# Causal attention in a transformer block: the 256-column parts of two neighbouring groups of heads share a unit

## The chip, the cores and the metric

The kernel runs on one core of a Trainium2 chip. The metric is the device time of one execution in microseconds (us); several executions give a median. A profile is one further execution in which every instruction of each engine was recorded. The engines are TensorE (PE; its weight loads are shown as PEld), VectorE (DVE), ScalarE (ACT), GpSimd (POOL) and SyncE (SP), which issues the transfers. "L1372" is line 1372 of the kernel.

## The reference

Eight sequences of 1024 tokens with 512 features go through one transformer block whose normalizations are modulated by a condition. Cut to what matters:

```python
mod = silu(condition) @ Wada + bada
sh_a, sc_a, gt_a, sh_m, sc_m, gt_m = split(mod, 6, axis=1)
xm = layernorm(x, g1, be1) * (1 + sc_a) + sh_a
q, k, v = split_heads(xm @ Wqkv)                    # 16 heads of 32
scores = einsum('bhqd,bhkd->bhqk', q, k) * 32 ** -0.5
scores = where(causal, scores, -inf)
x = x + gt_a * (softmax(scores) @ v @ Wproj + bproj)
xm = layernorm(x, g2, be2) * (1 + sc_m) + sh_m
x = x + gt_m * (gelu(xm @ W1 + b1) @ W2 + b2)
```

All inputs and the output are float32. The causal mask lets a token see itself and what is before it.

## The kernel before

**Tiling.** The 8 sequences are cut in two halves of 512 tokens, which gives 16 blocks n = (b, h). A block with h = 0 attends to its own keys, one with h = 1 also to those of the half before it. The 16 heads of 32 features are four groups g of four heads. A group's queries and keys lie with features on the partitions, 32 for each head, so its four heads are multiplied at once on four row tiles of TensorE (32 rows, 128 columns: the forms "32*128"). The linear layers, the values and the sums use four column tiles instead ("128*32"), and the transposes the whole array ("128*128"). float32 matmuls show as two instructions each in the trace.

**Units of attention.** The scores are made twice. A *score unit* (scores, here mostly scores_at_once, L1372) has queries on the partitions. It fills the PSUM tile "st" of four heads by 512 columns; VectorE adds the mask on the diagonal squares (L1384) and takes the maximum of each row (L1392). When a group's last score unit is done, split_maxima splits its maxima into three bf16 numbers (four small operations, L1411 to L1414, on VectorE or GpSimd, as the planner decides), and maxima_rows lays them out as a row (TensorE L1430, ScalarE copy L1436). A *weight unit* (weights_T) has keys on the partitions: the products again (L1456), then the maxima are subtracted by bf16 matmuls with a row of minus ones (L1467), ScalarE takes the exponential (L1479) into one of three SBUF buffers pT, and GpSimd zeroes what lies above the diagonal (affine_select, L1484). weigh multiplies by the values into the PSUM tile "po" (L1507), and additions (L1611, some on VectorE in the last group, L1608) gather the weights into the group's first pT, from which finish makes the sums (L1525), their reciprocals and the quotient. Scores and weights share the one PSUM tile "st", so each unit waits until the engine that reads the one before it is done.

**The triangle.** On the diagonal block of 512 by 512 only the lower triangle of 128-wide strips is computed. Its four strips have 512, 384, 256 and 128 columns and are packed in three units: [0], [1, 3] and [2], that is 512, 384 + 128, and 256 alone (TRIANGLE). A group has three units of each kind in a block with h = 0, and seven (four full ones first) with h = 1.

**Order.** Nothing is scheduled by the compiler: the program is written out in order by a planner at build time. It keeps an estimated clock per engine (now), and for each buffer when it is written and left (note, note_pe, note_act). Linear work (projections q, k, v, output projection, the two MLP layers, all Strassen products) runs as threads of small steps; before an attention unit, step_aside lets such steps go first while the unit would wait, and pace sets how far the linear work should be. attend walks through slots: slot k of group g makes weight unit k, closes the unit before it (values and, at the end, the sums), adds weights, and then makes as many score units of the next group as `upto` says. The buffers' queue free_p hands out three pT; a group's first one is kept until its sums are made. SyncE issues weight pieces in the order in which the linear steps will need them, as buffers of a ring of nine come free, with the loads of x, of the gate rows (row_ga and others, L493) and the stores between them. The output projection (project_out) of block n takes its first gate product on VectorE from row_ga.

Of the kernel before, what the change touches and what calls it, by code (L numbers as in the profile page):

```python
# [22 lines left out]
def kernel(  # L23
# [33 lines left out]
    nc = tc.nc  # L57
# [829 lines left out]
    def project_out(n):  # L887
# [8 lines left out]
        if last:  # L896
            for t in range(NTT):
                written["att", n, t] = NEVER
# [379 lines left out]
    def score_units(n, g):  # L1278

        h = blocks[n][1]  # L1280
        whole = [[(qt, kh, 0, TB)] for kh in range(h) for qt in range(NTT)]
        for tri in TRIANGLE:
            parts, at = [], 0
            for i in tri:
                w = TB - i * P
                parts.append((NTT - 1 - i, h, at, w))
                at += w
            whole.append(parts)
        return [(n, g, parts) for parts in whole]

    def weight_units(n):

        h = blocks[n][1]
        whole = [[(k, 0, TB)] for k in range(h * NTT)]
        for tri in TRIANGLE:
            parts, at = [], 0
            for i in tri:
                parts.append((h * NTT + i, at, TB - i * P))
                at += TB - i * P
            whole.append(parts)  # L1300
        return whole
# [13 lines left out]

    def scores(n, g, parts):

        h = blocks[n][1]
        if (n, g) not in maxima:
            maxima[n, g] = small.tile([P, 2, NTT, HPG], F32, tag="mx", name=f"mx_{n}_{g}")  # L1320
        mx = maxima[n, g]
        reads = [("qT", n), ("kT", n - h + parts[0][1])]
        if (
            linear_wait() > 3000
            and not any(live)
            and wait_of((reads, ["st"])) > wait_of((reads, [BANK])) + 1000
        ):
            scores_by_heads(n, g, parts, mx, reads)
        else:
            scores_at_once(n, g, parts, mx, reads)  # L1330
        if units[unit_at[0] + 1 :] == [] or units[unit_at[0] + 1][:2] != (n, g):
            split_maxima(n, g, h)

    def scores_by_heads(n, g, parts, mx, reads):

        h = blocks[n][1]
        for some in (range(HPG - 1), range(HPG - 1, HPG)):
            step_aside(reads, [BANK])
            of = {j: lin_bank() for j in some}
            for qt, kh, c0, w in parts:  # L1340
                for j, bank in of.items():
                    r = slice(j * hd, (j + 1) * hd)
                    nc.tensor.matmul(
                        banks[bank][:, c0 : c0 + w],
                        qTs[n][r, g, ts(qt, P)],
                        keys_of(n, kh)[r, g, :w],
                        start=True,
                        stop=True,
                        skip_group_check=True,
                    )  # L1350
                note_pe(2 * COLUMN * w, "rows", reads, [("l", bank) for bank in of.values()])
            for j, bank in of.items():
                if parts[0][1] == h:
                    first, span = parts[0][3] - P, len(parts) * P
                    diagonal = banks[bank][:, first : first + span]
                    nc.vector.tensor_tensor(diagonal, diagonal, mask[:, :span], ALU.add)
                    note("DVE", 120 + 1.04 * span, [("l", bank)])
                for qt, kh, c0, w in parts:
                    nc.vector.tensor_reduce(
                        mx[:, kh, qt, j : j + 1], banks[bank][:, c0 : c0 + w], axis=AX.X, op=ALU.max  # L1360
                    )
                    note("DVE", 170 + w, [("l", bank)], [("mx", n, g)])
                live[bank] = False

    def scores_at_once(n, g, parts, mx, reads):
# [3 lines left out]
        for qt, kh, c0, w in parts:  # L1369
            for j in range(HPG):  # L1370
# [3 lines left out]
                    qTs[n][r, g, ts(qt, P)],  # L1374
                    keys_of(n, kh)[r, g, :w],
# [5 lines left out]
        if parts[0][1] == h:  # L1381
            first, span = parts[0][3] - P, len(parts) * P
            diagonal = sc[:, :, first : first + span]
            nc.vector.tensor_tensor(  # L1384
                diagonal,
                diagonal,
                mask[:, :span].unsqueeze(1).to_broadcast([P, HPG, span]),
                ALU.add,
            )
            note("DVE", 165 + 4.16 * span, ["st"])  # L1390
        for qt, kh, c0, w in parts:
            nc.vector.tensor_reduce(  # L1392
                mx[:, kh, qt, :], sc[:, :, c0 : c0 + w], axis=AX.X, op=ALU.max
            )
            note("DVE", 170 + 4.14 * w, ["st"], [("mx", n, g)])
# [48 lines left out]
    def weights_T(n, g, parts):  # L1444
# [3 lines left out]
        row = m_rows[n, g]  # L1448
        reads = [("qT", n), ("kT", n), ("mrow", n, g)]
        step_aside(reads, ["st"])  # L1450
        st = ps_st.tile([P, HPG, TB], F32, tag="st", name=f"st_{n}_{g}_{parts[0][0]}")
        for k, c0, w in parts:
            kT = keys_of(n, k // NTT)
            for j in range(HPG):
# [3 lines left out]
                    kT[r, g, ts(k % NTT, P)],  # L1458
                    qT[r, g, TB - w :],
# [4 lines left out]
        for k, c0, w in parts:  # L1464
# [16 lines left out]
        if parts[0][0] >= h * NTT:  # L1481
            for _, c0, _ in parts:
# [13 lines left out]
    def weigh(n, g, parts, pT, slot, last):  # L1496
# [6 lines left out]
        for k, c0, w in parts:  # L1503
# [61 lines left out]

    def attend():
        previous = None
        for n in range(NB):
            h = blocks[n][1]
            t_units = weight_units(n)  # L1570
            n_slots = len(t_units)
            slots = []
            mine = sum(exp_need(parts) for parts in t_units) * NC
            for g in range(NC):
                nxt = groups.index((n, g)) + 1
                for k in range(n_slots):
                    upto = len(units)
                    if nxt < len(groups):
                        lo, m = first_unit[groups[nxt]], len(score_units(*groups[nxt]))
                        upto = lo + min(m, -(-(k + 2) * m // n_slots))  # L1580
# [4 lines left out]
                    slots.append((g, k, upto))  # L1585
            mine += sum(score_need(*unit) for unit in units[unit_at[0] : slots[-1][2]])
# [3 lines left out]
            for g, k, upto in slots:  # L1590
                parts = t_units[k]
# [8 lines left out]
                if k > 0:  # L1600
                    acc, first = totals[n, g]
                    for _, c0, w in parts:
                        for j in range(HPG):
                            into = acc[:, j, TB - w :]
                            keys = [("p", slot)], [("acc", n, g), ("p", first)]
                            if j % 2 and (n, g) == groups[-1]:

                                nc.vector.tensor_tensor(into, into, pT[:, j, c0 : c0 + w], ALU.add)  # L1608
                                note("DVE", 150 + 2 * w, *keys, port=True)
                            else:  # L1610
                                nc.gpsimd.tensor_tensor(into, into, pT[:, j, c0 : c0 + w], ALU.add)  # L1611
                                note("POOL", 230 + 2.07 * w, *keys)
# [16 lines left out]
    def close(n, g, parts, pT, slot, last):  # L1629

        until(lambda: n - blocks[n][1] + parts[-1][0] // NTT in valued)
        weigh(n, g, parts, pT, slot, last)
        if parts[0][0] == 0:
            totals[n, g] = (pT, slot)
        else:
            free_p.append(slot)
# [15 lines left out]
    def score_need(n, g, parts):  # L1652
        ns = 300 + sum(100 + 2100 * w / TB for _, _, _, w in parts)
# [3 lines left out]
    needs = sum(exp_need(parts) for n in range(NB) for parts in weight_units(n)) * NC  # L1657
    needs += sum(score_need(*unit) for unit in units)
    for n in range(NB):
# [5 lines left out]
        if n > 2:  # L1665
            written["free for k", n] = NEVER
    normalize(x_pre.pop(0), "a0", [("x", "a0")] * NTT)
# [67 lines left out]
```

## Time and profile before

| | |
|---|---|
| median of three runs | 3648.94 us (3645.09 to 3651.8) |
| the profiled execution | 3647.89 us |
| its span, first to last instruction | 3646.2 us |
| mean granted TensorE clock | 0.995 |
| exponentials of 2048 and of 1024 elements | 256 and 64, mean 1.879 and 1.025 us |
| reductions of 2048, 1536, 1024 and 512 elements | 191, 63, 64 and 63, mean 2.291, 1.758, 1.225 and 0.681 us |
| additions of weights, 512, 384, 256 and 128 columns (GpSimd) | 504, 254, 254 and 254, mean 1.308, 1.045, 0.750 and 0.459 us |

The span is what the trace covers; the time of an execution lies a little above it. In the profile a group of instructions is one line, engine, operation and set of tiles, with the count, the busy time, the mean of one in ns, and the idle time of its engine just before it. A wait belongs to the instruction that came last to release it. Matmuls overlap in the pipeline, so the time that one takes is read from start to start, not from its length.

### The profile page before, as it was taken

Reading aid. Unit: us, or ns where it says so; the run is one execution under the profiler, and the core shown is the slowest. Engines: PE = TensorE matmul, PEld = TensorE weight load, DVE = VectorE, ACT = ScalarE, POOL = GpSimd, SP = SyncE. Lnnn points to the kernel's source line nnn. Section 1 sums busy time; section 2 is a strip of 40 time slices with the busy share of each in tenths; the row PEclk is TensorE's granted clock in tenths of the full one; section 3 lists DMA queues with packets and bytes.
Section 4 is the critical chain, followed back from the end, with each engine's and each line's share of the span. In section 5 each row is a group of like instructions: output and inputs, shape, how many; then the busy total and the mean of one; then the engine's idle time right before and its main releaser. Section 6 shows DMA issues by size and latency. Waiting matters only on the chain. (4 is left out here: it accounts for less than half of the span.)

```text
span 3646.2 us, 121167 instructions
## 1 busy us (share of the span) xinstructions
PE 3571.6 (98%) x54821; PEld 1770.1 (49%) x54821; DVE 2179.1 (60%) x2501; ACT 1329.2 (36%) x1413; POOL 2014.6 (55%) x2039
## 2 busy tenths in 40 slices
PE   8999999999999999999999999999999999999999
PEld 4434445445554455544545444454544545445445
DVE  6766675564746557465564656746667465664663
ACT  2335234252333523335242352424524244241431
POOL 3656645656455664566636665456654566544560
PEclk9999999999999999999999999999999999999999
DMA  6623333333333343433434334343333433334334
GB/s 220 225 92 104 104 103 109 123 106 119 114 115 112 106 126 111 134 94 104 126 106 143 91 100 123 106 137 103 97 122 110 140 100 103 117 97 143 92 107 138
DMA packets 307894, 430.35 MB, mean 118 GB/s; under 512 B 25900, under 2 KB 176236, under 8 KB 307380
## 3 DMA queue, kind: packets, MB, share of 16 engines
q1 hardware_dynamic: 307264, 422.56, 37.9%
q8 instruction: 432, 7.08, 0.8%
q14 instruction: 82, 0.67, 0.1%
q10 hardware_dynamic: 116, 0.03, 0.0%
HBM read 394.12 MB, written 28.38 MB: 116 GB/s over the span
## 5 line engine op out<-in xcount | busy, mean ns | idle before, releaser
L1611 POOL TENSOR_TENSOR pT<-pT,pT 128x512 f32<-128x512 f32 (+3 forms) x1266 | 1189.2, 973 | 524.9 <-ACT pT L1479 377.1
L1479 ACT ACTIVATE pT<-st 128x2048 f32<-128x2048 f32 (+1 forms) x320 | 546.5, 1708 | 951.3 <-PE st L1467 909.0
L201 PE MATMUL bank<-w,hT 128*32 128x256 f32 x14336 | 808.6, 380 | 2.8 <-DVE hT L1006 2.1
L1392 DVE TENSOR_REDUCE mx<-sc 128x4 f32<-128x1024 f32 (+3 forms) x381 | 664.4, 1757 | 192.4 <-PE sc L1372 185.8
L201 PEld LDWEIGHTS bank<-w,hT 128*32 128x32 f32 x14336 | 452.1, 110 | 354.0 <-issue 58.0
L201 PE MATMUL bank<-xm_m,w 128*32 128x256 f32 x8192 | 506.6, 380 | 0.6 <-ACT rec L1531 0.5
L1484 POOL TENSOR_SCALAR_AFFINE_SELECT pT<-pT 128x512 f32<-128x512 f32 x256 | 175.3, 696 | 576.9 <-ACT pT L1479 576.9
L201 PE MATMUL bank<-t_m,w 128*32 128x256 f32 x6144 | 383.2, 380 | 0.9 <-ACT hT L188 0.9
L201 PEld LDWEIGHTS bank<-xm_m,w 128*32 128x32 f32 x8192 | 253.3, 110 | 252.0 <-issue 98.0
L1456 PE MATMUL st<-qT,kT 32*128 32x512 f32 (+3 forms) x3072 | 339.6, 526 | 21.0 <-DVE mx L1392 20.0
L1372 PE MATMUL sc<-kT,qT 32*128 32x256 f32 (+3 forms) x3048 | 340.6, 527 | 2.9 <-DVE mx L1392 1.9
L1384 DVE TENSOR_TENSOR sc<-sc,mask 128x1024 f32<-128x1024 f32 (+1 forms) x191 | 166.7, 873 | 248.5 <-PE sc L1372 225.5
L1507 PE MATMUL po<-pT,v 128*32 128x512 f32 (+3 forms) x3072 | 312.7, 493 | 2.2 <-POOL pT L1484 1.2
L201 PEld LDWEIGHTS bank<-t_m,w 128*32 128x32 f32 x6144 | 191.9, 110 | 175.7 <-issue 54.2
L201 PE MATMUL bank<-xm_a,w 128*32 128x256 f32 x3968 | 243.5, 381 | 0.0
L201 PE MATMUL bank<-w,qT 128*32 128x512 f32 x2048 | 241.1, 597 | 0.4 <-DVE qT L1547 0.2
L1540 DVE RECIPROCAL rec<-rec 128x128 f32<-128x128 f32 x256 | 224.6, 919 | 8.5 <-ACT rec L1531 8.5
L1456 PEld LDWEIGHTS st<-qT,kT 32*128 32x128 f32 x3072 | 128.9, 184 | 182.7 <-issue 57.5
L1372 PEld LDWEIGHTS sc<-kT,qT 32*128 32x128 f32 x3048 | 126.8, 184 | 161.0 <-ACT pT L1479 77.4
L193 DVE TENSOR_TENSOR hT<-bank,u_u 128x512 f32<-128x512 f32 x192 | 130.2, 686 | 120.9 <-PE bank L201 116.7
L201 PE MATMUL bank<-t_a,w 128*32 128x256 f32 x2944 | 187.2, 382 | 0.0
L1479 ACT ACT_TABLE_LOAD x89 | 114.2, 1283 | 189.3 <-PE st L1467 188.6
(205 smaller groups left out, 3589.5 us busy)
## 6 DMA issues: line engine op xcount, KB each, us to landing
w<-in_L_cond_W_dram SPq DMA_DIRECT2D x384, 256.0 KB, 2.9
w<-kept_up_S SPq DMA_DIRECT2D x256, 256.0 KB, 2.6
w<-kept_down_S SPq DMA_DIRECT2D x256, 256.0 KB, 2.7
w<-kept_qkv_S SPq DMA_DIRECT2D x180, 256.0 KB, 3.0
w<-in_L_cond_Wqkv_dram SPq DMA_DIRECT2D x147, 256.0 KB, 3.3
hat<-in_x_dram SPq DMA_DIRECT2D x64, 256.0 KB, 3.2
w<-in_L_cond_Wproj_dram SPq DMA_DIRECT2D x64, 256.0 KB, 3.8
xr<-in_x_dram SPq DMA_DIRECT2D x64, 256.0 KB, 4.2
```

What stands on the lines that cost most here:

```text
L193: nc.vector.tensor_tensor(out, src, other, op)
L201: nc.tensor.matmul(ps[r, :], lhsT[:, r], rhs, start=start, stop=stop, skip_group_check=True)
L1372: nc.tensor.matmul(sc[:, j, c0 : c0 + w], qTs[n][r, g, ts(qt, P)], keys_of(n, kh)[r, g, :w], start=True, stop=True, skip_group_check=True,)
L1384: nc.vector.tensor_tensor(diagonal, diagonal, mask[:, :span].unsqueeze(1).to_broadcast([P, HPG, span]), ALU.add,)
L1392: nc.vector.tensor_reduce(mx[:, kh, qt, :], sc[:, :, c0 : c0 + w], axis=AX.X, op=ALU.max)
L1456: nc.tensor.matmul(st[:, j, c0 : c0 + w], kT[r, g, ts(k % NTT, P)], qT[r, g, TB - w :], start=(c0 == 0), stop=False, skip_group_check=True,)
L1479: nc.scalar.activation(pT[:, :, :used], st[:, :, :used], AF.Exp, scale=scale)
L1484: nc.gpsimd.affine_select(diagonal, diagonal, pattern=[[0, HPG], [1, P]], compare_op=ALU.is_ge, fill=0.0, base=0, channel_multiplier=-1,)
L1507: nc.tensor.matmul(po[r, TB - w :], v[:, k % NTT, g * P + j * hd : g * P + (j + 1) * hd], pT[:, j, c0 : c0 + w], start=(k == 0), stop=last ...
L1540: nc.vector.reciprocal(some, some)
L1611: nc.gpsimd.tensor_tensor(into, into, pT[:, j, c0 : c0 + w], ALU.add)
```

## The change

The third unit of the triangle, 256 columns, is no longer a unit of its own in each group. Groups with even g make one unit of 512 columns out of their own 256 and those of group g + 1, for the scores and for the weights; groups with odd g have one unit fewer of each kind. A part carries its group as a last entry. In the shared score unit the mask reaches the diagonal squares of both parts in one operation (diagonals), and each part has its own reduction. In the shared weight unit each part subtracts the maxima of its own group, so the row of group g + 1 must be there by then; attend makes its score units one slot earlier in even groups (`over`), and calls for the row if it isn't made. One exponential takes both parts. The values and the additions of the second part are kept in `shared` and done when the first unit of group g + 1 is closed, and the pT buffer is freed only then. The mark that the last block's quotients aren't written yet is set at the start. Row counts of the planner (mine, needs) follow. The diff without the changes that only carry the new entry along:

```diff
@@ score_units
-        whole = [[(qt, kh, 0, TB)] for kh in range(h) for qt in range(NTT)]
+        whole = [[(qt, kh, 0, TB, g)] for kh in range(h) for qt in range(NTT)]
...
+            if tri == [2]:
+                if g % 2:
+                    continue
+                parts.append((*parts[0][:2], at, w, g + 1))
             whole.append(parts)
@@ weight_units(n, g)
+            if tri == [2]:
+                if g % 2:
+                    continue
+                parts.append((parts[0][0], at, TB - 2 * P, g + 1))
             whole.append(parts)
@@
+    def diagonals(parts, sc):
+        if parts[-1][4] == parts[0][4]:
+            first, span = parts[0][3] - P, len(parts) * P
+            return span, sc[:, :, first : first + span]
+        return 2 * P, sc.rearrange("p j (a c) -> p j a c", c=2 * P)[:, :, :, P:]
@@ scores_at_once
+            span, place = diagonals(parts, sc)
+            shape_of = mask[:, :span].unsqueeze(1)
+            if len(place.shape) == 4:
+                shape_of = shape_of.rearrange("p o (a c) -> p o a c", c=P)
+            nc.vector.tensor_tensor(place, place, shape_of.to_broadcast(place.shape), ALU.add)
...
+        for qt, kh, c0, w, gg in parts:
+            nc.vector.tensor_reduce(
+                maxima[n, gg][:, kh, qt, :], sc[:, :, c0 : c0 + w], axis=AX.X, op=ALU.max
+            )
@@ weights_T
-        reads = [("qT", n), ("kT", n), ("mrow", n, g)]
+        reads = [("qT", n), ("kT", n)] + [("mrow", n, gg) for gg in {part[3] for part in parts}]
@@ attend
+                n_slots = len(weight_units(n, g))
+                over = n_slots - 1 if g % 2 == 0 else n_slots
...
-                        upto = lo + min(m, -(-(k + 2) * m // n_slots))
+                        upto = lo + min(m, -(-(k + 2) * m // over))
...
+                parts = weight_units(n, g)[k]
+                while rows_due and any((n, part[3]) not in m_rows for part in parts):
+                    maxima_rows()
                 pT, slot = weights_T(n, g, parts)
...
+                    add_weights(n, g, [part for part in parts if part[3] == g], pT, slot)
@@ close
-        weigh(n, g, parts, pT, slot, last)
+        own, other = [[part for part in parts if (part[3] == g) == of] for of in (True, False)]
+        weigh(n, g, own, pT, slot, last)
+        if other:
+            shared[n, g + 1] = other, pT, slot
+        elif parts[0][0] > 0:
+            free_p.append(slot)
         if parts[0][0] == 0:
             totals[n, g] = (pT, slot)
-        else:
-            free_p.append(slot)
+            if (n, g) in shared:
+                more, pT, slot = shared.pop((n, g))
+                weigh(n, g, more, pT, slot, False)
+                add_weights(n, g, more, pT, slot)
+                free_p.append(slot)
@@ project_out, and before the first step
-        if last:
-            for t in range(NTT):
-                written["att", n, t] = NEVER
+    for t in range(NTT):
+        written["att", NB - 1, t] = NEVER
```

add_weights is the loop of additions that stood in attend, for the parts that it is given.

## The prediction

> **What bounds the kernel now.** First the page's engine row: TensorE is busy 98% of the span, the next engine (VectorE) 60%.
>
> ```profile
> span 3646.2 us, 121167 instructions
> PE 3571.6 (98%) x54821; PEld 1770.1 (49%) x54821; DVE 2179.1 (60%) x2501; ACT 1329.2 (36%) x1413; POOL 2014.6 (55%) x2039
> ```
>
> So time is won only by giving TensorE less to do or less to wait for. What it waits for is in the waits view of PE (total us, times, longest), some 69 us over 22 rows. Its largest row and the one row of the tail are:
>
> ```profile
> PE st L1456 <- DVE mx L1392: 20.0, 35, 1.9
> ...
> PE bank L1525 <- POOL pT L1611: 1.6, 1, 1.6
> ```
>
> The rest is work, but busy is not streaming. The timeline of PE (start, length, engine, line, count) shows what one unit costs beyond its columns; the lengths overlap, so I subtract starts.
>
> ```profile
> 3440.84 1.05 PE L201 MATMUL bank<-t_m,w 128*32 128x256 f32 x16
> 3441.70 0.61 PE L201 MATMUL bank<-w,hT 128*32 128x256 f32 x8
> 3442.25 1.14 PE L1372 MATMUL sc<-kT,qT 32*128 32x512 f32 x8
> ...
> 3468.45 0.71 PE L1372 MATMUL sc<-kT,qT 32*128 32x256 f32 x8
> 3469.09 2.37 PE L201 MATMUL bank<-w,hT 128*32 128x256 f32 x40
> 3471.39 0.71 PE L1456 MATMUL st<-qT,kT 32*128 32x256 f32 x8
> 3471.92 0.29 PE L1467 MATMUL st<-mrow,minus_ones 32*128 32x256 bf16 x4
> 3472.14 2.15 PE L201 MATMUL bank<-w,hT 128*32 128x256 f32 x36
> ...
> 3479.00 8.38 PE L201 MATMUL bank<-w,hT 128*32 128x256 f32 x152
> 3487.20 1.04 PE L1525 MATMUL bank<-pT,ones 128*32 128x512 f32 x8
> ```
>
> Pace: 152 matmuls in 8.20 us, 54 ns for one of 256 columns. Leaving column tiling (128*32): 24 matmuls would take 1.295 us, the row-tiled unit (32*128) starts after 1.41: 0.115 us. A row-tiled stretch: eight matmuls stream 0.43 us, the next stretch starts after 0.64: 0.21 us; with the four bf16 ones 0.54 of 0.75, again 0.21. The 512-wide score units take the same (3442.25 to the next column matmul at 3443.32 is 1.07, streaming 0.86). So a unit of scores or weights costs 0.325 us whatever its width. Transposes have such a price too:
>
> ```profile
> 717.18 0.33 PE L641 MATMUL bank<-ident,xh_m 128*128 128x128 f32 x1
> 717.44 0.64 PE L201 MATMUL bank<-t_a,w 128*32 128x256 f32 x8
> ```
>
> One transpose streams 0.107 us (128 columns), the next matmul comes after 0.26: 0.15 us.
>
> **The change, part by part.** *Merged units.* 64 groups of heads had 64 score and 64 weight units of 256 columns; 32 and 32 of 512 are left. Columns streamed are the same, so 64 x 0.325 = 20.8 us go. The trace of before has no such unit, so the price is bounded by 0.325 (as for the 384-and-128 unit, two parts) and 2 x 0.325; I take the first, the nearer row. All of this is on TensorE, with nothing beside it that could hide it.
>
> *Order.* The planner places everything anew, so I counted the built order of TensorE in both kernels. Stretches, before to after: row-tiled 636 to 571, column 682 to 607, transposes 93 to 50, with equal matmuls. Transposes now run together where linear work used to cut them. Priced by the rows above: 65 x 0.21 = 13.7, 75 x 0.115 = 8.6, 43 x 0.15 = 6.5: 28.8 us, of which 20.8 are the edit's and 8 the new order's.
>
> *VectorE.* The groups by form:
>
> ```profile
> L1392 DVE TENSOR_REDUCE mx<-sc 128x4 f32<-128x1024 f32 x64 | 78.4, 1225 | 2.2
> L1384 DVE TENSOR_TENSOR sc<-sc,mask 128x512 f32<-128x512 f32 x128 | 89.3, 698 | 172.3 <-PE sc L1372 158.0 <-issue 13.8 <-ACT hat L580 0.3
> L1384 DVE TENSOR_TENSOR sc<-sc,mask 128x1024 f32<-128x1024 f32 x63 | 77.5, 1230 | 76.3 <-PE sc L1372 67.5 <-ACT rec L1531 4.4 <-ACT top L1534 1.9
> ```
>
> A merged score unit has one mask over eight stretches of 128 and two reductions. The 0.698 row is already four such stretches, so the mask is between 1.23 and 1.40; I take 1.23. The unit holds the one PSUM buffer for 1.23 + 2 x 1.225 = 3.68 us, where a 256 unit held it 1.92; the sum per pair falls from 3.84. ScalarE: one exponential of 2048 (1.88) for two of 1024 (2.05). GpSimd's selections and additions stay in number; those of the second part move behind the next group's first slot. The built order also moves the four small operations that split the maxima to GpSimd in nearly every group (there each takes 0.25, on VectorE 0.40 to 0.91). None of these is on TensorE's path: VectorE, ScalarE and GpSimd are idle 40%, 64% and 45%. Without that cover, see the slower rival.
>
> *New waits.* The shared weight unit also needs the next group's row of maxima, so its scores are due a slot earlier; on TensorE everything queues behind. In the last block (the built order) 2.6 us of other columns stand between that row's transposes and the first matmul that reads it, and the copy needs what is left of an exponential (about 0.6) and 0.58: covered. The shared weights keep their buffer one slot longer; the exponential two slots on waits for GpSimd's four additions (4 x 0.75), on an engine idle 45%: nothing here, and up to 3.0 us at each of 32 if GpSimd were behind.
>
> *Waits gone or come, from the trace's places and the new order.* (a) Of the 20.0 us, 13 waits recur with the blocks (seven of 0.88, six of 0.73: 10.5 us), behind a reduction with too few columns after it; in the new order those places have more columns. Minus 10.5. (b) A new place, seven times (once for each pair of blocks after the first): a 384-and-128 score unit follows a masked 512 one after 2.15 us of columns, and needs 0.2 + 0.70 + 2.29 and a VectorE busy some 0.3 us: 1.0 x 7 = plus 7. (c) Output projection of each even block: its first gate on VectorE waits for the copy of a gate row:
>
> ```profile
> 663.67 0.69 DVE L193 TENSOR_TENSOR y<-bank,row_ga 128x512 f32<-128x512 f32 x1 [0.75 <-DMA row_ga<-kept_ga]
> ```
>
> That is 6.3 us after the projection began (657.3). SyncE issues as many DMAs as before (1518 rows in both built orders), four loads of x, then the gate rows, behind the values' last weights, so the row lands at the same distance. But now a reduction stands behind that gate, and the next weight unit behind the reduction. By the durations gate at +6.7, addition +7.5, reduction +8.3 to +10.6; the unit is reached at about +11. Slack 0.4 us; a copy later by 3 us costs nearly as much. Bounds 0 and 3.5 us for each, seven places; I take 1.0, near the lower end, where the landing of the trace puts it: plus 7. (d) Tail: the 1.6 us before the last sums goes; before it the new order has 11 us of columns for an exponential, two selections and four additions (1.88 + 1.3 + 3.0). After it 8.6 us more stand before the projection, which cover the copy and first reciprocals. Minus 1.6. The last unit of all is now a 512 one; that is counted here. (e) Start: the first h=1 block works through single banks with long waits; one more score unit goes that way. Zero, plus or minus 6.
>
> Sum: -28.8 - 10.5 + 7 + 7 - 1.6 = -26.9. Against the profiled execution, 3647.89 us (span 3646.2 and 1.7 around it), that is 3621; the median shown is 1.05 above it: **3622 us**.
>
> [...] At the start the trace shows what waits do to the clock, in the row of stretches (us, then PE, PEld, DVE, ACT, POOL, clock, DMA share, GB/s):
>
> ```profile
> 183.00:190.00 7.00, 6.39 (x22) 2.70 (x26) 6.83 (x15) 0.00 (x0) 0.64 (x3) 0.50 0.99 310
> ```
>
> This stretch, full of matmuls, follows a wait of 3.66 us and runs at half clock; from 210 to 240 the clock is 1.00, and no later wait is longer than 3.0. [...] By the row, with waits under 3 us, the sum stands. [...]
>
> **Rivals.** *The units shrink but waits take back part*: (c) at 2.5, (e) at +6, (a) half kept: -28.8 - 5 + 7 + 17.5 + 6 - 1.6 = -5 at the worst, -15 in the middle, 3634. For it: slack of 0.4 us. Against it: reductions cost PE 20 us over some 318 score units. *Slower: the PSUM buffer.* One buffer serves scores and weights, and a merged score unit holds it 1.76 us longer. [...] If TensorE stands w us longer at each of the 32 merged score units, the sum is -26.9 + 32w: it decides from w = 0.84, and with the whole 1.76 uncovered it is +29, 3678. Against it: the 64 short units and 63 of 384 and 128 columns (which hold the buffer 3.67 us already) cost little in PE's waits, and where the merged unit is its group's last, the split on GpSimd (4 x 0.25 against some 2.5 on VectorE) gives back most of the 1.76.
>
> *It doesn't do what it says*: if each part pays the 0.325 and not each unit, nothing goes but the 8 us of the order, and with (a) to (d) -6, 3643. Against it: the score unit of 384 and 128, two parts, costs the same as one part (start 3458.46 to the next column matmul 3459.54: 1.08, streaming 0.86).
>
> **Chances and range.** Forecast 0.68 (3610 to 3632), part taken back 0.21 (3632 to 3641), unchanged 0.04, slower by the buffer 0.07. A difference of 0.2%, 7.3 us, is about what a measurement of this kernel tells from none. Faster 0.89, same 0.04, slower 0.07. Range 3610 to 3638: the lower end is (b) and (c) at zero with a better start, the upper takes in most of the second case; little more than 0.1 is left above.
>
> **What would show it.** Busy PE falls by about 29 us; 64 fewer row-tiled units with 0.21 + 0.115 us each, a 256+256 unit 0.21 over its 0.86 us; transposes in about 50 stretches. The row of waits for reductions stays near 17 us plus (c); a wait at the second weight group of even-block projections shows (c). I am wrong if merged units cost 0.43 over streaming, if that wait is 3 us or more seven times, or if PE's waits for reductions of scores pass 45 us.

## The result and the profile after

| | before | after |
|---|---|---|
| median | 3648.62 us (3645.09 to 3651.8, 4 runs) | 3615.12 us (3611.87 to 3619.6, 4 runs) |
| ratio to before | | 0.991, 95% interval 0.9898 to 0.9922 |
| the profiled execution and its span | 3647.89, 3646.2 us | 3611.87, 3610.1 us |
| mean granted TensorE clock | 0.995 | 0.995 |

The change takes 33.5 us away; 26.9 were forecast (to 3622), and 3615 lies inside the range. The engine row of the page, after:

```profile
span 3610.1 us, 121129 instructions
PE 3537.6 (98%) x54821; PEld 1777.0 (49%) x54821; DVE 2078.8 (58%) x2316; ACT 1325.9 (37%) x1388; POOL 2038.3 (56%) x2187
```

PE has the same 54821 matmuls and is busy 34.0 us less (3571.6 before), of a span that is 36.1 us shorter. So almost all of it is work that got cheaper, and little of it is waits. The timeline of PE (start, length, line, count) has the new unit, which before lacked:

```profile
1680.99 1.15 PE L1389 MATMUL sc<-kT,qT 32*128 32x256 f32 x16
1682.07 1.93 PE L201 MATMUL bank<-t_m,w 128*32 128x256 f32 x32
```

From start to start it takes 1.08 us. Its 512 columns stream 0.86, and 0.22 is left: one price for two parts. Measured as below, with half clock left out, and taken by form, 31 shared score units and 32 shared weight units cost 0.21 us each, and so do the single units of 256 columns before (62 and 56) and the units of 512.

The waits view of PE (total us, times, longest), after:

```profile
PE po L1521 <- POOL pT L1498: 10.2, 6, 2.1
PE bank L1357 <- DVE mx L1376: 10.1, 3, 4.5
PE sc L1389 <- DVE mx L1406: 7.0, 7, 1.0
PE bank L409 <- ACT cond_act L403: 6.4, 1, 6.4
PE st L1469 <- DVE mx L1406: 5.0, 7, 1.6
```

The row that was largest, weight units behind a reduction, went from 20.0 us in 35 places to 5.0 in 7. In its place stand the values behind a triangle selection (10.2; 1.2 before), the scores behind a reduction (7.0; 1.9 before) and the scores made head by head at the start (10.1; 4.3 before).

To see where TensorE's time went I cut its timeline into stretches of one tiling (row tiles 32*128, column tiles 128*32, transposes 128*128). Of each stretch I took the time from its start to the start of the next, less its columns at the pace of the prediction (54 ns for 256, half of that for bf16, 107 ns for a transpose), and less idle time that the trace shows. What is left is the cost beyond streaming. Every kernel streams the same columns, so the differences do not hang on that pace. In some stretches the granted clock is 0.5, and half of the time then counts as cost; the fourth column says how much of the column-tiled cost this is (in the row-tiled it is 6.5 to 9.3 everywhere). Stretches: us beyond streaming; the last columns are PE's idle time and the span:

| kernel | row-tiled | column-tiled | of it half clock | transposes | idle | span |
|---|---|---|---|---|---|---|
| before | 636: 145.0 | 684: 108.7 | 2.4 | 92: 26.7 | 70.5 | 3646.2 |
| after | 571: 130.9 | 608: 95.8 | 5.0 | 49: 18.9 | 68.4 | 3610.1 |
| after, repeated | 571: 130.6 | 608: 100.3 | 9.8 | 49: 19.6 | 66.6 | 3613.2 |
| shared scores alone | 605: 135.8 | 648: 105.2 | 4.7 | 76: 24.2 | 77.8 | 3638.6 |
| shared weights alone | 601: 137.1 | 668: 121.4 | 15.3 | 103: 27.4 | 116.9 | 3699.0 |
| shared weights alone, splits on GpSimd | 601: 138.5 | 661: 111.0 | 9.6 | 94: 23.2 | 78.7 | 3646.7 |
| after, parts cut apart | 633: 143.3 | 662: 103.5 | 1.9 | 63: 22.0 | 63.0 | 3627.2 |
| before, strips 384 and 128 apart | 763: 173.2 | 793: 128.2 | 7.2 | 73: 27.1 | 77.8 | 3701.9 |
| before, transposes in one go | 636: 145.0 | 673: 110.7 | 4.7 | 64: 20.7 | 62.8 | 3634.5 |
| before, later additions | 636: 144.5 | 683: 109.0 | 1.4 | 92: 24.9 | 62.2 | 3636.9 |
| before, both of these | 636: 144.1 | 671: 106.2 | 2.2 | 65: 20.8 | 50.7 | 3618.9 |
| after, later additions | 571: 131.4 | 608: 94.5 | 5.0 | 49: 19.2 | 56.5 | 3597.0 |
| after, splits on VectorE | 572: 128.8 | 608: 101.4 | 8.7 | 49: 18.0 | 76.1 | 3620.6 |

After against before: row-tiled -14.1, column-tiled -12.9, transposes -7.8, idle -2.1, together -36.9 for 36.1 of span (the last stretch of each kernel is left out). The counts are those of the trace, one or two off the built order.

### The profile page after: what moved, and what is told of

It is laid out like the page before. It is cut to its first block, busy times and chain, and to the rows that moved or that the text cites. A ratio compares the mean times of both kernels' runs of the same rounds, so it can differ in the third digit from the quotient of the medians.

```text
span 3610.1 us, 121129 instructions
## 1 busy us (share of the span) xinstructions
PE 3537.6 (98%) x54821; PEld 1777.0 (49%) x54821; DVE 2078.8 (58%) x2316; ACT 1325.9 (37%) x1388; POOL 2038.3 (56%) x2187
## 4 chain that ended last, share of the span: by engine, by line
PE 90%; DVE 4%; POOL 2%; ACT 2%; issue 1%; DMA 0%; SPq 0%; ACTq 0%; DVEq 0%; POOLq 0%
PE bank L201 62%; PE st L1469 8%; PE sc L1389 8%; PE po L1521 7%; DVE mx L1406 2%; PE st L1481 2%; PE bank L641 2%; PE bank L1539 2%; POOL pT L1594 1%; POOL xr L161 1%; ACT pT L1493 1%; DVE hT L1003 0%; PE bank L1444 0%; DVE xr L158 0%; ACT hT L945 0%
## 5 line engine op out<-in xcount | busy, mean ns | idle before, releaser
L1594 POOL TENSOR_TENSOR pT<-pT,pT 128x384 f32<-128x384 f32 (+2 forms) x1266 | 1195.6, 981 | 400.4 <-PE po L1521 211.0
L1493 ACT ACTIVATE pT<-st 128x2048 f32<-128x2048 f32 x288 | 541.0, 1878 | 858.2 <-PE st L1481 826.5
L1406 DVE TENSOR_REDUCE mx<-sc 128x4 f32<-128x2048 f32 (+3 forms) x380 | 658.5, 1754 | 147.7 <-PE sc L1389 140.6
L201 PE MATMUL bank<-xm_m,w 128*32 128x256 f32 x8192 | 498.3, 381 | 3.1 <-ACT xm_m L651 3.0
L201 PE MATMUL bank<-t_m,w 128*32 128x256 f32 x6144 | 392.2, 381 | 0.4 <-DVE t_m L660 0.4
L1498 POOL TENSOR_SCALAR_AFFINE_SELECT pT<-pT 128x512 f32<-128x512 f32 x256 | 162.1, 651 | 400.4 <-ACT pT L1493 400.4
L1389 PE MATMUL sc<-kT,qT 32*128 32x512 f32 (+3 forms) x3040 | 331.6, 524 | 7.6 <-DVE mx L1406 7.0
L1469 PE MATMUL st<-qT,kT 32*128 32x512 f32 (+3 forms) x3072 | 330.9, 523 | 6.7 <-DVE mx L1406 5.0
L1521 PE MATMUL po<-pT,v 128*32 128x512 f32 (+3 forms) x3072 | 305.8, 493 | 10.2 <-POOL pT L1498 10.2
```

What stands on the lines that cost most here:

```text
L201: nc.tensor.matmul(ps[r, :], lhsT[:, r], rhs, start=start, stop=stop, skip_group_check=True)
L1389: nc.tensor.matmul(sc[:, j, c0 : c0 + w], qTs[n][r, gg, ts(qt, P)], keys_of(n, kh)[r, gg, :w], start=True, stop=True, skip_group_check=True,)
L1406: nc.vector.tensor_reduce(maxima[n, gg][:, kh, qt, :], sc[:, :, c0 : c0 + w], axis=AX.X, op=ALU.max)
L1469: nc.tensor.matmul(st[:, j, c0 : c0 + w], kT[r, gg, ts(k % NTT, P)], qT[r, gg, TB - w :], start=(c0 == 0), stop=False, skip_group_check=True,)
L1493: nc.scalar.activation(pT[:, :, :used], st[:, :, :used], AF.Exp, scale=scale)
L1498: nc.gpsimd.affine_select(diagonal, diagonal, pattern=[[0, HPG], [1, P]], compare_op=ALU.is_ge, fill=0.0, base=0, channel_multiplier=-1,)
```

## The experiments

Each kernel was timed beside the kernel before on the same chip; a ratio is to that one, with its 95% interval. All of them compute the whole reference.

**Repeat.** The changed kernel once more, as the base of its own variants.

> The changed kernel once more, beside the others on one chip: 33 us below the kernel before (ratio 0.991), as measured already. It is the mark for the next three.

Measured: 3616.16 us, ratio 0.9909 (0.9895 to 0.9923). As expected.

### One half of the change alone

**Shared score units, weights as before** (an edit to the changed kernel, in weight_units and attend):

```diff
-            if tri == [2]:
-                if g % 2:
-                    continue
-                parts.append((parts[0][0], at, TB - 2 * P, g + 1))
...
-                over = n_slots - 1 if g % 2 == 0 else n_slots
+                over = n_slots
```

> Score units shared as in the change, weight units as before. Built order: row-tiled stretches 636 to 605, column 682 to 649, transposes 93 to 77. Theory (each stretch has its price, 0.21, 0.115, 0.15 us): 31 x 0.21 + 33 x 0.115 + 16 x 0.15 = 12.7 us below before, 3636, if waits stay. Rival (the gain is in the weights, whose unit has the bf16 matmuls and the exponential): under 4 us below.

Measured: 3643.95 us, ratio 0.9986 (0.9977 to 0.9995), 5.4 below before, between the two expectations. The table says why: 31 fewer row-tiled stretches and their neighbours give -15.2, and idle time takes back 7.3. Two rows of its waits view:

```profile
PE po L1517 <- POOL pT L1494: 14.4, 10, 2.0
PE st L1465 <- DVE mx L1402: 11.7, 18, 1.4
```

Waits behind reductions fall from 20.0 to 11.7, and 14.4 us of values behind a selection appear. So this new wait doesn't need the shared weight units.

**Shared weight units, scores as before** (the same block taken out of score_units):

```diff
-            if tri == [2]:
-                if g % 2:
-                    continue
-                parts.append((*parts[0][:2], at, w, g + 1))
```

> Weight units shared, score units as before. Built order: row-tiled 636 to 601, column 682 to 665, transposes 93 to 104. Theory: 35 x 0.21 + 17 x 0.115 - 11 x 0.15 = 7.7 us below before, 3641. Rival (a unit is a unit, the order of transposes costs nothing): 35 x 0.325 = 11.4 us below, no less than the run with scores alone.

Measured: 3698.09 us, ratio 1.0136 (1.0123 to 1.015): 48.8 slower than before, with 35 row-tiled stretches fewer. Both expectations fail. Idle time is 46.4 us up, and the 12.7 us more in the column-tiled stretches are half clock (15.3 against 2.4). Three rows of its waits view:

```profile
PE bank L1440 <- DVE mcols L1424: 27.1, 7, 4.3
PE st L1465 <- DVE mx L1402: 18.2, 16, 2.9
PE sc L1385 <- ACT pT L1489: 11.0, 7, 1.7
```

The row of maxima waits for the last operation of the split. One of these seven places in the timeline of all engines (start, length, engine, line; in brackets the idle time and its releaser):

```profile
852.58 5.61 POOL L161 TENSOR_TENSOR hT<-hT,hT 128x1024 f32<-128x1024 f32 x2 [6.65 <-DVE hT L1003]
...
855.61 0.33 DVE L1421 CAST mcols<-mx 128x16 bf16<-128x16 f32 x1
...
855.98 2.25 DVE L1422 TENSOR_TENSOR rest<-mx,mcols 128x16 f32<-128x16 f32 x1
...
858.15 4.65 POOL L161 TENSOR_TENSOR hT<-hT 128x1024 f32<-128x1024 f32 x2
858.33 2.22 DVE L1423 CAST mcols<-rest 128x16 bf16<-128x16 f32 x1
...
860.59 2.29 DVE L1424 TENSOR_TENSOR mcols<-rest,mcols 128x16 bf16<-128x16 f32 x1
...
862.93 0.62 PE L1440 MATMUL bank<-ident_b,mcols 128*32 128x128 bf16 x16 [4.31 <-DVE mcols L1424]
```

Three operations on 16 numbers a partition take 2.2 to 2.3 us each, where the first took 0.33. The second and the fourth end just after additions of GpSimd that run beside them (858.23 after 858.19, 862.88 after 862.80). The planner had put the split on VectorE here; it reckons with 2.2 us there for all four operations, against 1.0 on GpSimd (the 2200 and 1000 in the next diff).

**The same, the split always on GpSimd.** If that is the cause, the loss must go with it:

```diff
-        on_pool = max(now["POOL"], ready) + 1000 < max(now["DVE"], ready) + 2200
+        on_pool = True
```

> The run with shared weight units alone once more, with the four small operations of each split of the maxima always on GpSimd. That run took 3698, and its trace shows seven waits of 4.3 us for the split on VectorE where the next group's row is due a slot earlier. Theory (the earlier row is the cost, and VectorE's queue makes it): those waits go, at least 7 x 4 = 28 us, 3660 to 3670. Rival (the row is late by the scores, not by the split): over 3685.

Measured: 3648.57 us, ratio 0.9996 (0.9986 to 1.0005), 49.5 below the kernel it was made from. The rival falls, and more goes than the theory's 28: the whole excess goes with the engine of the split (idle time -38.2, column-tiled stretches -10.4, of which 5.7 is half clock, transposes -4.2). But the shared weight units alone still gain nothing. The row for the maxima keeps 22.8 us, now behind splits on GpSimd:

```profile
PE bank L1440 <- POOL mcols L1424: 22.8, 15, 2.5
PE st L1465 <- DVE mx L1402: 16.4, 13, 1.8
```

A shared weight unit needs the row of group g + 1 early. The shared score unit yields the last maxima of both groups at once, which may be why this row is gone when both halves are made together; that is argued, no run isolates it.

**The changed kernel, the split always on VectorE** (63 of its 64 splits are on GpSimd, 22 before). Does it owe its gain to that?

```diff
-        on_pool = max(now["POOL"], ready) + 1000 < max(now["DVE"], ready) + 2200
+        on_pool = False
```

> The changed kernel with the splits always on VectorE (in its trace 63 of 64 are on GpSimd). The prediction says that GpSimd gives back most of the longer chain (4 x 0.25 against some 2.5 us). Built order: tiling stretches as in the changed kernel. Theory: waits for the rows of maxima of 1 to 4 us in many of the 56 places after the start, 20 to 60 us above the changed kernel. Rival (the planner finds enough other columns): within 6 us.

Measured: 3621.81 us, ratio 0.9925 (0.9911 to 0.9938), 5.7 above the repeat: the rival is right, narrowly. Its waits view:

```profile
PE bank L201 <- DVE hT L193: 13.7, 6, 2.6
...
PE bank L1444 <- DVE mcols L1428: 5.3, 3, 2.5
```

The split is late in three places only (5.3 us; 27.1 in seven with shared weights alone). Elsewhere in this order of work TensorE had other columns to do meanwhile. The engine of the split is a hazard that the change happens to avoid; at most 5.7 us of its gain come from there.

### The price of a unit

**Parts cut apart.** The shared units stay (buffers, masks, exponentials), but TensorE does one step of linear work between their two parts:

```diff
+    def cut():
+        at = spent[0]
+        while spent[0] == at and threads() and linear_wait() < 300:
+            work()
...
         for qt, kh, c0, w, gg in parts:
+            if gg != g:
+                cut()
```

and the same in the first loop of weights_T.

> The changed kernel with a step of linear matmuls put between the two parts of each shared unit: VectorE, ScalarE and GpSimd keep their merged operations, TensorE gets its tiling changes back. Built order: row-tiled 571 to 633, column 607 to 662, transposes 50 to 64. Theory (the tiling changes are the gain): 62 x 0.21 + 55 x 0.115 + 14 x 0.15 = 21.4 us above the changed kernel. Rival (the gain is fewer operations and waits on the other engines): within 6 us of the changed kernel.

Measured: 3628.92 us, ratio 0.9947 (0.9935 to 0.996), 12.8 above the repeat, between the two. The 62 stretches that came back cost 12.7 us, 0.20 each. Column stretches, 54 more, cost 3.2, and transposes, cut again by the linear steps (49 to 63), 2.4. Idle time fell by 3.6, which hid part of it, and half clock hid more: the repeat lost 9.8 us to it in its column stretches, this run 1.9. Without half clock the three cost 13.4, 11.1 and 3.0, that is 27.5 us and no less than the theory's 21.4.

**The opposite.** The strips of 384 and 128 columns, one unit before, each as its own:

```diff
-    TRIANGLE = [[0], [1, 3], [2]]
+    TRIANGLE = [[0], [1], [3], [2]]
```

(with the mark for the last block's quotients set at the start, as in the change).

> The kernel before with the strips of 384 and 128 columns as units of their own (four units of each kind per group on the triangle, the columns the same; the mark on the last block's quotients set at the start, as in the change). Built order: row-tiled stretches 636 to 763, column 682 to 793, transposes 93 to 74. Theory: 127 x 0.21 + 111 x 0.115 - 19 x 0.15 = 36.6 us above before, 3685, more if the short units bring waits. Rival (the price is by columns or by part): within 8 us of before.

Measured: 3704.87 us, ratio 1.0156 (1.014 to 1.0171), 56 above before: the rival is out, and the theory's 36.6 is too small. Row-tiled stretches: 28.2 us for 127 more, 0.22 each. Column-tiled: 19.5 for 109, 0.18, of which 4.8 us is half clock (0.13 without it). Transposes: 0.4 more, where 2.9 less were forecast. Idle time: 7.3 more. The row price is that of the prediction (0.21), the column price without half clock not far from it (0.115); waits and half clock stood in no term.

### The order

**Transposes in one go.** In the new order transposes stand together. That is to be had without the change, in modulated:

```diff
-        yield [("hat", key, 0), *guards], [BANK]
+        yield [*(("hat", key, t) for t in range(NTT)), *guards], [BANK]
...
-                if t:
-                    yield [("hat", key, t)], []
```

> The kernel before with the transposes of one block and chunk made in one go, waiting for all four normalized tiles first; attention is untouched. Built order: row-tiled 636 as before, column 682 to 671, transposes 93 to 65. Theory: 28 x 0.15 + 11 x 0.115 = 5.5 us below before, less what waiting for the fourth tile costs. Rival (transposes cut by other work cost nothing by themselves): no change, or slower by the longer wait.

Measured: 3637.48 us, ratio 0.9969 (0.9958 to 0.9981), 11.4 below before, twice the forecast. 28 fewer transpose stretches give -6.0 (0.21 each), and idle time falls by 7.7, for which the forecast had no term. This is not idle time in front of the transposes (12.0 us before, 12.3 here). It is the row of weight units behind reductions, which was 20.0:

```profile
PE st L1454 <- DVE mx L1390: 12.2, 20, 1.8
```

One of its places in the kernel before:

```profile
937.08 0.77 PE L641 MATMUL bank<-ident,xh_m 128*128 128x128 f32 x5
938.72 1.15 PE L1456 MATMUL st<-qT,kT 32*128 32x384 f32 x16 [0.88 <-DVE mx L1392]
```

Seven such waits of 0.88 us stood right behind transposes. In this run none of them is left, and the six of 0.73 are all still there. The edit was not run in the changed kernel, whose transposes stand in 49 stretches already.

### The new wait

In the changed kernel values wait for a selection that GpSimd does late. One of the four long places in the timeline of all engines:

```profile
1687.03 6.22 POOL L161 TENSOR_TENSOR xr<-xr,row_gbm 128x512 f32<-128x512 f32 x3
...
1687.57 1.88 ACT L1493 ACTIVATE pT<-st 128x2048 f32<-128x2048 f32 x1 [6.77 <-PE st L1481]
1687.61 4.52 DVE L1003 TENSOR_TENSOR hT<-hT 128x1024 f32<-128x1024 f32 x2
...
1693.20 0.63 POOL L1498 TENSOR_SCALAR_AFFINE_SELECT pT<-pT 128x512 f32<-128x512 f32 x1
...
1693.89 1.67 PE L1521 MATMUL po<-pT,v 128*32 128x512 f32 x8 [2.06 <-POOL pT L1498]
```

The exponential was done at 1689.45 (1687.57 + 1.88), but three gate additions stand before the selection in GpSimd's queue until 1693.2. They take 2.07 us each beside VectorE's additions (1.28 where none runs beside; see the end). The price goes on after the wait, as the stretches show (us; PE, PEld, DVE, ACT, POOL busy; clock; DMA share; GB/s):

```profile
1691.00:1693.90 2.90, 0.84 (x23) 0.17 (x11) 2.83 (x4) 2.87 (x4) 2.83 (x3) 1.00 0.28 81
1693.90:1696.00 2.10, 2.10 (x16) 0.78 (x20) 0.00 (x0) 2.10 (x3) 2.08 (x2) 0.57 0.04 14
1696.00:1700.00 4.00, 4.00 (x52) 1.82 (x44) 0.00 (x0) 1.54 (x3) 4.00 (x5) 0.80 0.22 61
```

The clock falls to 0.57 and 0.80 where TensorE is busy throughout: 0.43 x 2.1 + 0.20 x 4 = 1.7 us lost. The trace's record of the clock has 0.5 for 3.41 us from 1694.21, which gives the same. It happened at two of the four places in this execution, at all four in the repeat. Two more at 1.7 are part of what makes the repeat's span 3.1 us longer; other stretches at half clock and waits differ too.

**Later additions, in the changed kernel.** The gate additions go behind the copy of the next product:

```diff
-            for i in range(NTT):
-                add_to(residual[n][:, i, :], gate_rows["gbm"], [("row", "gbm")], [("xr", n, i)])
             combine(nc.vector, "B12", "B12", "B11")
...
             copy_out(got["u1"], bank, ps, [key("u1")])
+            for i in range(NTT):
+                add_to(residual[n][:, i, :], gate_rows["gbm"], [("row", "gbm")], [("xr", n, i)])
```

> The changed kernel with the four additions of the gate row to the residual (the first of the four parts of the second MLP layer) issued after that part's first product, so that they no longer stand on GpSimd ahead of a triangle selection. Theory (the waits of the values for that selection, 10.2 us in 6 places, come from those additions): 6 to 10 us below the changed kernel, 3606, and the row of PE's waits for L1498 nearly gone. Rival (something else takes the place): within 3 us of it.

Measured: 3598.33 us, ratio 0.9862 (0.9849 to 0.9876), 17.8 below the repeat and 50 below the kernel before: the best version of this study, and twice what was expected. Its waits view, from the top, and a stretch at the same place:

```profile
PE bank L1357 <- DVE mx L1376: 9.9, 3, 4.5
PE sc L1389 <- DVE mx L1406: 7.0, 7, 1.0
...
PE po L1521 <- POOL pT L1498: 1.8, 1, 1.8
```

```profile
1690.00:1700.00 10.00, 10.00 (x168) 5.12 (x161) 4.04 (x5) 8.02 (x9) 9.87 (x11) 1.00 0.30 81
```

The row of the selection fell from 10.3 us in six places to 1.8 in one, the four long places are gone, and here the clock stays at 1.00. Idle time fell by 10.1 us and time beyond streaming by 5.4. Of that, half clock is 4.5: the 4 x 1.7 = 6.8 of the repeat's four places went, and 2.3 came elsewhere.

**The same in the kernel before.** Does it only undo what the change brought?

> The kernel before with the later gate additions that made the changed kernel 17 us faster (and the mark on the last quotients set at the start, as in the change). Built order: tiling stretches as before. If those additions only undid a wait that the change brought in: within 3 us of before, 3646 to 3652. If they are a gain of their own: 8 us or more below.

Measured: 3639.7 us, ratio 0.9974 (0.9964 to 0.9984), 9.6 below: a gain of its own, in a kernel where that wait was 1.2 us. PE's idle time fell by 8.3. What the edit mends there is a different set of short waits: those behind reductions fall from 20.0 to 17.5, and rows of 3.0, 2.1 and 1.2 us are gone. So the 17.8 can't be read whole as the price of the change's new wait, though in the changed kernel the trace puts 8.5 us on that row and 6.8 on half clock behind it.

**Both edits in the kernel before**, to see what the shared units are worth when the order is helped without them:

> The kernel before with whole transposes and with later additions, attention untouched: what can be had without shared units. Theory: the two add up, 11 us from whole transposes and the gain of the run with later additions alone, 3630 to 3638, and the shared units are worth what then is missing to 3598, 32 us or more. Rival (shared units gave mostly the order of transposes): below 3612.

Measured: 3622.8 us, ratio 0.9928 (0.9916 to 0.9941), 26.5 below before, between the two expectations; the two edits give more together than their sum (11.4 + 9.6). The changed kernel with later additions, whose transposes stand together already, is 24.5 below it, and not 32. Between these two kernels the stretches differ by 65 row-tiled (-12.7), 63 column-tiled (-11.7) and 16 transposes (-1.6), and idle time by +5.8. Without the later additions in either kernel it is 33.2 - 11.4 = 21.8 us. So some 22 to 24 us are the shared units' own, the waits that they bring counted in, and the rest of the 33 came with the new order.

## Why the prediction was right, and where its steps were off

**Merged units, 20.8 us: right, priced low on one term.** A merged unit takes one price, 0.21 to 0.22 over its streaming, as the first of the two bounds had it; the rival in which each part pays its own is out. The row-tiled term held (0.21 forecast, 0.20 to 0.22 in four comparisons). The column-tiled term, 0.115, was read at one clean place. With half clock taken out, a column stretch in which TensorE did not wait costs 0.13 us, the median of 570 to 740 stretches in each of seven kernels. One in which it waited costs some 0.3 beyond the wait itself (a single one of 4.5 left out). From before to after 61 of the first kind went (-9.5 us) and 15 of the second (-6.0). So the price was nearly right, and what the term lacked is that a wait also costs something after it.

**New order, 8 us: right in kind, too small.** The counts came as built. All stretches together gave -34.8, forecast -28.8: column-tiled -12.9 (8.6; 15.5 less 2.6 more half clock), row-tiled -14.1 (13.7), transposes -7.8 (6.5). The run with transposes in one go shows that this last gain needs no shared unit. What makes the planner put them together in the new order stays open.

**(a) Waits behind reductions, -10.5: right, larger.** 20.0 to 5.0. Of the 13 waits that were counted, the seven of 0.88 go when only the transposes are put together, so they belong to the order and not to the shared units. The six of 0.73 stay in that run. With shared scores alone 11.7 us remain.

**(b) A 384-and-128 score unit behind a masked 512 one, +7: right to the tenth.** 7.0 us in 7 places, longest 1.0. The 1.0 is the sum without the 0.3 us that the step allows for a busy VectorE; with them its terms come to 1.3.

**(c) The gate row's copy, +7: wrong, it cost nothing.** The timeline of all engines at the place, after:

```profile
658.58 0.69 DVE L193 TENSOR_TENSOR y<-bank,row_ga 128x512 f32<-128x512 f32 x1 [5.95 <-PE bank L201]
...
659.36 0.89 DVE L158 TENSOR_TENSOR xr<-xr,y 128x512 f32<-128x512 f32 x1
...
660.17 2.27 DVE L1406 TENSOR_REDUCE mx<-sc 128x4 f32<-128x2048 f32 x1
...
663.03 1.14 PE L1469 MATMUL st<-qT,kT 32*128 32x512 f32 x8
```

The gate waits for its product and not for the copy; the reduction ends at 662.44, and the weight unit comes at 663.03. The slack is 0.6 us (forecast 0.4), and the copy comes in time. Once in the run, at 3278 us, the gate did wait 2.6 us for the transfer. The value taken should have been the lower bound.

**(d) The tail, -1.6: right.** The wait before the last sums is gone. A wait of 0.9 us for the reciprocals came in its place.

**(e) The start, 0 within 6: right in size, at its upper end.** The scores made head by head wait 10.1 us in three places, 4.3 before.

**Not foreseen: values behind a selection, +9, and half clock after it.** No term stood for it. The nearest, the wait for the shared pT, was put at "nothing here, and up to 3.0 us at each of 32 if GpSimd were behind". GpSimd was behind, through three gate additions and not through the weights' own additions. The step looked at GpSimd's idle share, 45%, where its queue at that place was what mattered. The clock was also read too loosely: "waits under 3 us" were taken as safe, and a wait of 2.06 us was followed by 3.41 us at half clock. The trace of before spoke against it: it has 6.8 us at half clock from 3347 and again from 3538, and no wait near them is longer than 2.3 us. Nor does the stretch from 183 to 190 us show what the wait of 3.66 us did to the clock, for the clock had been at half since 176.4, before that wait began.

**VectorE, ScalarE: right.** The mask of a shared unit was put at 1.23 and the reductions at 1.225. Groups by form, after (count | busy us, mean ns | idle time before):

```profile
L1403 DVE TENSOR_TENSOR sc<-sc,mask 128x1024 f32<-128x1024 f32 x95 | 116.9, 1231 | 175.0 <-PE sc L1389 147.8 <-issue 15.6 <-ACT hat L580 9.5
...
L1406 DVE TENSOR_REDUCE mx<-sc 128x4 f32<-128x1024 f32 x64 | 75.3, 1218 | 1.1
...
L1428 POOL TENSOR_TENSOR mcols<-rest,mcols 128x16 bf16<-128x16 f32 x63 | 19.3, 307 | 5.0
```

The first row holds 63 masks of 384-and-128 units and the 32 of the shared units, with one mean, 1.231. The split took 0.23 to 0.31 an operation on GpSimd. The slower rival, PSUM held longer by a merged score unit, would show as weight or score units behind reductions; those two rows together fell from 21.9 to 12.0.

**The sum.** Terms forecast: -28.8 of stretches and +1.9 of waits. Measured: -34.8 and -2.1. In the waits, -15.0 (a), +5.1 (b, with the 1.9 that such waits had before), 0 (c), -1.6 (d), +5.8 (e) and +9.0 (selection) give +3.3; the small rows are the other -5.4, which no step had. That the waits came out near their forecast is luck: the 7 us of (c) that did not come, the 4.5 more of (a) and the small rows stand against the selection and the start.

## What to carry to other kernels

Where TensorE is busy 98%, count the changes of tiling in the built order of both kernels: each row-tiled stretch cost 0.21 us and each column-tiled one 0.13 where nothing waited, whatever the columns, and the counts foretold most of the gain. A change that goes through a planner also moves everything else, so its halves need not add up: one gave -5.4, the other +48.8, both together -33.5, and the loss of the second lay wholly in the engine that four tiny operations were placed on. For each wait, look at what stands in the queue of the releasing engine at that place; its idle share over the span says little, and edits that reorder that queue (17.8 us here) can be worth half as much as the change under study. Before a difference of some us is explained, take half clock out of both traces: two executions of the changed kernel differed by 5.6 us in it.

## What the hardware showed that was not expected

**Half clock after a wait of 2 us, at some places and not at others.** TensorE was busy 0.84 of 2.90 us, the wait itself was 2.06 us, and then 3.41 us ran at half clock. The same wait left the clock alone at two of four places in one execution and at none of four in the other. The record of the clock in the trace of after, without the first 10 and the last 5 us, is at 0.5 in seven stretches:

| start, us | 178.69 | 185.52 | 250.37 | 397.14 | 1694.21 | 3021.99 | 3506.69 |
|---|---|---|---|---|---|---|---|
| length, us | 3.41 | 13.65 | 6.83 | 3.41 | 3.41 | 3.41 | 3.41 |

All their beginnings and ends lie whole multiples of 3.413 us apart, to within 0.01 us. So do those of the three in the trace of before (176.36, 3347.34 and 3538.49 us, for 23.89, 6.83 and 6.83), and those in each of the 13 traces, counted from a different point in each. Cut into such steps, two of the four places look like this, each with the step that holds the most of the wait and with what follows it:

```profile
1690.80:1694.20 3.40, 1.34 (x31) 0.49 (x28) 3.03 (x4) 3.37 (x4) 3.32 (x4) 1.00 0.26 77
1694.20:1697.60 3.40, 3.40 (x32) 1.43 (x28) 0.00 (x0) 3.34 (x5) 3.40 (x3) 0.50 0.00 0
...
2134.50:2137.90 3.40, 2.00 (x36) 1.01 (x32) 3.37 (x5) 3.36 (x5) 3.40 (x3) 1.00 0.05 12
2137.90:2141.40 3.50, 2.85 (x48) 1.48 (x52) 0.63 (x2) 3.50 (x4) 3.42 (x5) 1.00 0.19 68
```

The first step holds the whole wait, the other only 1.4 us of it, because it ends within the wait. I summed TensorE's idle time in each step from 200 us on, over all 13 traces, leaving out steps that ran at half clock already. Of the steps idle for 1.98 us or more, all 45 were followed by half clock (5 of 5 in the traces of before and after alone); of those between 1.85 and 1.98, 6 of 10 (1 of 3); between 1.0 and 1.85, 4 of 110 (1 of 15); below 1.0, none (none of 1969). So of the four waits of 2.06 us in the trace of after, the two with 2.06 us of idle time in one step were followed by 3.41 us at half clock, which cost 1.7 us, and the two with 1.45 and 1.88 us were not. Why the clock behaves so, no run shows.

**Operations of VectorE and GpSimd that ran beside each other took longer.** In the new wait's place three gate additions on GpSimd took 6.22 us, beside two of VectorE of 2.26 each. Where they don't overlap, an addition on GpSimd takes 1.28 (the median of 117 in the trace of after that had nothing of VectorE beside them) and the pair on VectorE takes 2.35 (the kernel with later additions). The ends alternate between GpSimd and VectorE, at 1688.83, 1689.92, 1691.04, 1692.12 and 1693.24 us, some 1.1 apart: near what one takes alone. In the kernel with shared weights alone VectorE's operations of the split, which can take 0.2 to 0.4 us (the last one 0.23, the median of 21), took 2.2 to 2.3 beside GpSimd's additions of 2.3 to 2.8. These are single places of single executions; that the engine of the split matters is shown by the run with the splits on GpSimd (49.5 us), why the operations took longer by none.
